# A graph layer with gathered rows: the first set's sorting spread over the table and the first fourteen parts

## The chip, the cores and the metric

The kernel runs on one core of one Trainium2 chip. The metric is device time in microseconds (us), the median of several runs. The engines are named as in the profile: PE is TensorE, DVE is VectorE, ACT is ScalarE, POOL is GpSimd, and SP is the engine that here only issues DMAs. PEld is PE's weight load.

## What is computed

The graph has 12,500 nodes with 128 features and 412,500 directed edges, sorted by destination. Each edge gets a weight from the difference of its ends; each node sums its weighted differences, adds a term in its in-degree, and the result is normalized.

```python
theta = x[dst] - x[src]
w = sigmoid(relu(theta @ W1 + b1) @ W2 + b2)
agg = segment_sum(w * theta, dst)
indeg = segment_sum(ones, dst)
out = layernorm(x + agg + indeg * (x @ W4 + b4))
```

## The kernel before

**Two stages.** The table stage computes `x @ W1` once for every node and writes rows of `x @ W1` and `x` side by side to DRAM (`z`). It walks over 14 chunks: twelve of 1,024 nodes, one of 128 and one of 84 (`table_chunk`, L598). For a chunk PE transposes eight tiles (L607), ACT copies them from PSUM (L610), PE multiplies (L612), DVE copies the product (L615), ACT copies `x` (L616), and SP writes the chunk to `z` (L617). The edge stage then walks over 372 parts of up to 1,024 edges, two parts to a block, so that a block shares a window of 96 destination nodes. I number parts and chunks from 0.

**A part.** POOL gathers the rows of the part's sources with eight indirect DMAs of 128 rows each (`gather`, L324 to L341; I call all eight "gather s"). Parts 0 to 7 (`NH` = 8) gather only `x`, so that they need not wait for `z`, and PE works out `x @ W1` for them in place (`both`, L728: transposes L735, ACT copies L737, products L740 and L742). Later parts gather from `z`. DVE forms one-hot matrices (L699 or L705 for the spreading of the window's values, L724 for the adding up), rectifies and reduces (L753 or L757 and L758, then L761), ACT forms the sigmoid and scales the rows (L762, L764), and PE adds them up by destination (L827). Per block, `window` (L651) and `part_y` (L664) compute the window's values: L655, L659, L660 and L672 on PE, copies L657, L662, L675 and L678 on ACT, L670, L676 and L680 on DVE.

**Gathers' pace.** There are nine row buffers (`zbuf`); two `x` parts share one. POOL takes the gathers strictly in order. Gathers 0 to 7 are held to the pace of the table. Gather 8 and later need all of `z`. Gathers 8 to 12 go into free buffers, gather 13 into the buffer of parts 0 and 1. From gather 14 on, each waits for a named PE instruction of the part six before it (`LAG` = 6): gather 14 for the last spreading matmul that part 8's turn issues (L714), and so on.

**Sorting.** Parts 0 to 17 (`PLAIN`) use the edges as they stand. The other parts are sorted in sets of 128 parts by the generator `place` (L425), which puts its work out in small steps; a `next(steps, None)` runs one. For one set there are 79 calls, in this order:

| calls | what they do | where |
|---|---|---|
| 1 | column constants | L434-449 |
| 2 to 4 | key, by thirds; each third holds the PSUM buffer `pw` | L453-464 |
| 5 to 7 | key, end | L467-479 |
| 8 to 23 | eight times the eight largest (L483), then their replacement (L485) | L481-485 |
| 24 | the list of frequent sources, its DMA on SP (L500), a matmul (L506) | L489-509 |
| 25 to 30 | counting, in sixths; each holds `pw` | L512-530 |
| 31 to 72 | shifting, 7 rounds of 6 strips; three DVE instructions a strip (L543, L545, L547) | L535-549 |
| 73, 74 | results out: DMA `off_d` (L557) on SP, three ACT copies | L551-565 |
| 75 to 79 | PE transposes (L571) and ACT copies (L573) into `src_i` and `rel` | L567-575 |

Set 0 holds parts 18 to 145. So gather 18 reads `src_i`, and part 18's one-hot reads `off_d` back from DRAM (`to_all`, L639).

**What sets the order.** All loops are unrolled. SP keeps the written order. For PE, DVE, ACT and POOL a scheduler fixes the order when the program is built, by its own estimate of when each instruction can run; on the chip every engine runs its list strictly in order. Buffers decide too: `pw` and `pd` are single PSUM buffers (2 KB a partition each), handed on in written order, and `pw` is used by the table's first four transposes, by `place`, by `window`, by `part_y` and by `both`. The strips' scratch `bits` (L205) lies in one PSUM tile, `fix`, with the row of numbers that L724 compares with and with `own` (written by ACT at L843, read by DVE at L848).

**Around the change.** Chunks 0 and 1 are emitted ahead of the loop at L914, so that loop runs for chunks 2 to 13. The loop over parts begins at L934; its line L944 decides how many steps of sorting each part carries.

Of the kernel before, what the change touches and what calls it, by code (L numbers as in the profile page):

```python
# [33 lines left out]
NH = 8  # L34
FIRST = P // K
MORE = 2
PLAIN = FIRST + MORE
# [11 lines left out]
def gnn_resnorm(  # L49
# [48 lines left out]
    chunks = [(n0, P, TC) for n0 in range(0, N - P * TC + 1, P * TC)]  # L98
# [34 lines left out]
    def load(i):  # L133

        s0, n, full = sets[i]
        es = ep.tile([P, CE], I32, name="es")
        ed = ep.tile([P, CE + 1], I32, name="ed")
        e0 = E1 + (s0 - PLAIN) * CE
        if full < n:
            nc.vector.memset(es[:n, :], 0)  # L140
            nc.vector.memset(ed[:n, :], N)
        for t, edges, m in ((es, src, CE), (ed, dst, CE + 1)):
            nc.sync.dma_start(t[:full, :m], bass.AP(
                tensor=edges.tensor, offset=edges.offset + e0, ap=[[CE, full], [1, m]]))
            if full < n:
                nc.sync.dma_start(
                    t[full:n, :TAIL], edges[E - TAIL:E].rearrange("(s e) -> s e", s=1))
        bb = ep.tile([P, 1], I32, name="bb")
        with nc.allow_non_contiguous_dma(reason="each block's first dst"):
            nc.sync.dma_start(bb[:n], bass.AP(  # L150
                tensor=dst.tensor, offset=dst.offset + e0, ap=[[SUB * CE, n // SUB], [0, SUB], [1, 1]]))
        return es, ed, bb
# [153 lines left out]
    def tiles(s):  # L306
        return K if s < NF else KT
# [16 lines left out]
    def gather(s):  # L324

        (src_i, _, _), i = set_of(s)
        for k in range(tiles(s)):
            ins = nc.gpsimd.indirect_dma_start(  # L328
                out=rows_of(s)[:, k, :], out_offset=None, in_=z if s >= NH else x,
                in_offset=IndirectOffsetOnAxis(ap=src_i[:, k, i:i + 1], axis=0))  # L330
            waits = [(gathers[-1], mybir.DependencyClass.NoSync)] if gathers else []
            at = (s * K + k) * 4 * len(chunks) // (NH * K) - 6
            if s < NH and 0 <= at < len(table_steps):
                waits.append((table_steps[at], mybir.DependencyClass.Sync))
            if s - LAG >= NH and (s - LAG, k) in steps_of:
                waits.append((steps_of[s - LAG, k], mybir.DependencyClass.Sync))
            for other, kind in waits:
                tc.add_manual_dep(
                    ins.ins, other.ins.name,
                    mybir.DependencyInfo(kind, mybir.DependencyReason.DATA), reason="gathers' pace")  # L340
            gathers.append(ins)  # L341
# [235 lines left out]
    with tc.manual_schedule(engines={SP}), tc.tile_pool(name="work", bufs=2) as wp, tc.tile_pool(  # L577
# [43 lines left out]
        @contextmanager  # L621
        def after(instructions):

            with ExitStack() as stack:
                for i in instructions:
                    stack.enter_context(tc.issue_after(i.ins))
                yield
# [23 lines left out]
        def window(b):  # L651

            d = blocks[b]
            pw = ps_l.tile([P, G, P], F32, name="pw")[:, 0, :]
            step(b * SUB - 4, 5, nc.tensor.transpose(pw[:, :WB], d["xw"][:WB], ident[:WB, :WB]))  # L655
            xwT = wp.tile([P, P], F32, name="xwT")
            nc.scalar.activation(xwT[:, :WB], pw[:, :WB], AF.Copy)  # L657
            pw = ps_l.tile([P, G, P], F32, name="pw")[:, :2, :]
            nc.tensor.matmul(pw[:WB], xwT[:, :WB], wts, start=True, stop=False)  # L659
            step(b * SUB - 4, 7, nc.tensor.matmul(pw[:WB, 1, :], ones_b[:, :WB], b4_3, start=False, stop=True))  # L660
            yu = yu_buf[b % len(yu_buf)]
            nc.scalar.activation(yu[:WB], pw[:WB], AF.Copy)  # L662
            d.update(u=yu[:, 1, :], yb=yu[:, 0, :])
            d["y3"] = part_y(b * SUB, SUB, d["yb"])  # L664
# [19 lines left out]
        def one_hot(s, half):  # L684


            n0, n1 = half * G, min(half * G + G, tiles(s))
            if half == 0:
                parts[s] = {"oh": oh_buf[s % 2]}
            oh = parts[s]["oh"]  # L690
            if s < PLAIN:
                (_, _, off), i = set_of(s)
                pd = ps_l.tile([P, G, P], F32, name="pd")
                pd = pd.rearrange("p k e -> p (k e)").bitcast(BF16)
                pd = pd.rearrange("p (k e) -> p k e", e=P)[:, :G, :]
                for k in range(n0, n1):
                    nc.tensor.transpose(pd[:, k - n0, :], off[:, k, i:i + 1].to_broadcast([P, P]),
                                        ident_b)
                nc.vector.tensor_scalar(oh[:3 * SW, n0:n1, :], pd[:3 * SW, :n1 - n0, :],  # L699
                                        place_c[:3 * SW], None, op0=OP.is_equal)  # L700
            elif half == 0:
                n = tiles(s)
                b, h = divmod(s, SUB)
                at = blocks[b]["to_all"].rearrange("p h (k e) -> p h k e", e=P)
                nc.vector.tensor_scalar(oh[:3 * SW, :n, :], at[:3 * SW, h, :n, :],  # L705
                                        place_c[:3 * SW], None, op0=OP.is_equal)
# [170 lines left out]
        def fetch(b):  # L877
            if b < NK:
                load_block(b)

        hot_blocks = range(PLAIN // SUB, NK)
        xts, done = [], []

        def chunk():
            c = len(done)
            xts.extend(table_load(i) for i in range(len(xts), min(c + 3, len(chunks))))
            done.append(table_chunk(c, xts[c]))
# [4 lines left out]
        def gather_first():  # L892

            while gathered[0] < AHEAD and (gathered[0] + 1) * len(chunks) <= (len(done) + 1) * NH:
                gather(gathered[0])
                gathered[0] += 1
# [17 lines left out]
        while len(done) < len(chunks):  # L914
            chunk()
            gather_first()
            with after(done[-1]):
                for _ in range(6):
                    next(steps, None)
        with after(done[7]):  # L920
            bases(FIRST, NS, ps_l)
# [12 lines left out]
        for s in range(NS + 2):  # L934
            if s in turns:
                edges[s + 3] = turns[s], load(turns[s])
            if s in edges:
                i, loaded = edges.pop(s)
                steps = place(i, ps_l, *loaded)
            if s == NH:  # L940
                nc.sync.dma_start(
                    hot_t, z[:HOT, :].rearrange("(p t) d -> p t d", t=HT))
                nc.scalar.activation(hot_t[:, :, :D], hot_t[:, :, :D], AF.Copy, scale=-1.0)
            if s % 2 == 0 or s < PLAIN - 3:  # L944
                for _ in range(3 if s < NH else 1):
                    next(steps, None)
            b = s // SUB
            if s % SUB == 0:
                fetch(b + 2)
                if b + 1 < NK:  # L950
                    window(b + 1)
            if s + AHEAD < NS:
                gather(s + AHEAD)
            if s >= NH and s + 2 < NS:
                one_hot(s + 2, 0)
            if s + 1 < NS:
                spread_y(s + 1)
            if s < NS - 1:
                one_hot_w(s)
            if s == NS - 2:  # L960
                one_hot_w(s + 1)
            if s < NS:
                weighted = weights(s)
            if s % SUB == 0 and b > 1:
                with after(weighted if s == NS else []):
                    normalize(b - 2)
            if s % SUB and b + 1 in hot_blocks:
                hot_weights(b + 1)
            if s < NH:
                one_hot(s + 2, 0)  # L970
            if s + 2 < NS and tiles(s + 2) > G:
                one_hot(s + 2, 1)
            if s % SUB == 0 and b + 1 in hot_blocks:
                hot_one_hot(b + 1)
            if s > 1:
                with after(weighted if s >= NS else []):
                    add_up(s - 2)
            if s % SUB == 0 and b + 1 in hot_blocks:
                hot_rows(b + 1)
            if s % 2 and s > PLAIN - 3:  # L980
                next(steps, None)
# [202 lines left out]
```

## Time and profile before

Three runs took 3914.03, 3919.13 and 3920.94 us. The profiled execution took 3919.01 us; its span, from the first instruction to the last, is 3917.2 us, so that 1.8 us lie outside.

| engine | busy us | share of the span | instructions |
|---|---|---|---|
| PE | 2667.6 | 68% | 15349 |
| PEld | 2252.2 | 57% | 15349 |
| DVE | 2829.5 | 72% | 5501 |
| ACT | 1594.4 | 41% | 5226 |
| POOL | 2866.5 | 73% | 2978 |

The mean granted PE clock is 0.81 of full speed. Some marks in the span, from the timelines of the engines:

| us from the span's start | what |
|---|---|
| 33.2 | DVE copies chunk 2 (L615) |
| 125.8 | DVE copies the last chunk (L615) |
| 136.3 | POOL issues the first DMA of gather 8 |
| 170.4 | ACT begins to read the sorted words (L565) |
| 179.9 | PE begins part 0 (L735) |
| 259.6 | POOL issues the first DMA of gather 14 |
| 301.6 | POOL issues the first DMA of gather 18 |
| 3889.4 | POOL issues the last DMA |

In the views, a line of a timeline gives start, duration, engine, line, operation, tiles and shapes, and in brackets the idle time before it with what ended it. A line of the waits gives the total, the number of times and the longest.

### The profile page before, as it was taken

To read this page: it belongs to the slowest core of one execution; us is meant where nothing else is said; L and a number is where in the kernel's file an instruction comes from. 1 tells how busy PE (TensorE), PEld (TensorE's weight loads), DVE (VectorE), ACT (ScalarE), POOL (GpSimd) and SP (SyncE) were. 2 spreads that over 40 slices of the span, in tenths; PEclk is the share of its full clock that TensorE was granted. 3 is DMA by queue.
4 is the path that set the end of the run, shared out by engine and by line. 5 is a ranking of instruction groups with operands and counts; after the bars stand their busy time and mean duration, and the time that the engine had idled before them with its cause. 6 is when DMAs were issued, how large, how long until landed. Compare 5 with 4: busy or idle time off the path is not lost.

```text
span 3917.2 us, 52459 instructions
## 1 busy us (share of the span) xinstructions
PE 2667.6 (68%) x15349; PEld 2252.2 (57%) x15349; DVE 2829.5 (72%) x5501; ACT 1594.4 (41%) x5226; POOL 2866.5 (73%) x2978
## 2 busy tenths in 40 slices
PE   3487776776667766667766776676766766767665
PEld 2366555555556655556555655566655656656554
DVE  6778787777767666669887777666666666666665
ACT  2254443434444343334444434444343443344443
POOL 3637777777777777777777777777777777777775
PEclk7698787877778888878887777878888888888887
DMA  5425444444444444445444444444445444444443
GB/s 179 138 66 163 138 138 142 142 144 143 139 143 143 142 143 142 133 143 150 143 140 138 142 141 146 142 139 139 141 142 144 142 141 138 142 143 144 141 136 98
DMA packets 242089, 547.83 MB, mean 140 GB/s; under 512 B 60819, under 2 KB 120893, under 8 KB 240129
## 3 DMA queue, kind: packets, MB, share of 16 engines
q0 software_dynamic: 141488, 385.15, 33.8%
q1 hardware_dynamic: 98335, 152.85, 12.9%
q10 hardware_dynamic: 1970, 6.40, 0.4%
q8 instruction: 123, 2.02, 0.2%
q14 instruction: 173, 1.42, 0.1%
HBM read 521.31 MB, written 22.85 MB: 139 GB/s over the span
## 4 chain that ended last, share of the span: by engine, by line
DVE 34%; DMA 22%; PE 19%; ACT 16%; issue 6%; POOL 2%; DVEq 0%; SPq 0%; ACTq 0%; POOLq 0%
DMA zbuf<-z,src_i 22%; PE pd L792 11%; ACT wx L764 10%; DVE ph L757 8%; DVE ph L758 8%; DVE lg L761 7%; PE pa L827 3%; ACT wx L762 2%; DVE of L779 2%; POOL zbuf L328 2%; DVE pw L676 1%; DVE ow L724 1%; PE pw L659 1%; ACT a L838 1%; DVE fix L848 1%
## 5 line engine op out<-in xcount | busy, mean ns | idle before, releaser
L328 POOL DMA_INDIRECT zbuf<-z,src_i x2825 | 2728.2, 966 | 860.9 <-issue 416.0
L792 PE MATMUL pd<-hot_t,of 128*128 128x256 f32 x3186 | 995.1, 482 | 187.5 <-DVE of L779 156.9
L757 DVE TENSOR_TENSOR ph<-ph,zbuf 128x1024 f32<-128x1024 f32 x364 | 446.7, 1227 | 846.3 <-DMA zbuf<-z,src_i 846.0
L792 PEld LDWEIGHTS pd<-hot_t,of 128*128 128x128 f32 x3186 | 777.8, 250 | 367.4 <-ACT wx L764 116.1
L827 PE MATMUL pa<-wx,ow 128*96 128x130 f32 x5938 | 905.6, 312 | 117.5 <-ACT a L838 109.3
L764 ACT ACTIVATE wx<-zbuf,wx 128x128 f32<-128x128 f32 x2969 | 910.8, 388 | 7.0
L827 PEld LDWEIGHTS pa<-wx,ow 128*96 128x96 f32 x5938 | 823.4, 192 | 153.6 <-ACT a L838 140.8
L714 PE MATMUL ph<-y,oh 128*128 128x128 bf16 x2905 | 292.5, 247 | 435.2 <-DVE y L680 287.6
L714 PEld LDWEIGHTS <-oh 128*128 128x128 bf16 x2905 | 236.4, 111 | 474.1 <-issue 342.1
L761 DVE TENSOR_REDUCE lg<-ph 128x8 f32<-128x1024 f32 x372 | 450.4, 1211 | 0.1
L758 DVE SCALAR_TENSOR_TENSOR ph<-ph,w_r 128x1024 f32<-128x1024 f32 x364 | 445.3, 1223 | 0.0
L838 ACT ACTIVATE a<-pa 96x130 f32<-96x130 f32 x186 | 50.4, 271 | 870.1 <-PE pa L827 870.0
L724 DVE TENSOR_TENSOR ow<-fix,rel 128x768 f32<-128x768 f32 x372 | 350.2, 942 | 12.0 <-ACT fix L843 5.9
L762 ACT ACTIVATE wx<-lg,b_c 128x8 f32<-128x8 f32 x372 | 112.2, 302 | 363.9 <-DVE lg L761 363.7
L779 DVE TENSOR_TENSOR of<-hot_all,fix 128x1152 f32<-128x1152 f32 x177 | 236.5, 1336 | 0.0
L678 ACT ACTIVATE ym<-pw 128x256 bf16<-128x256 f32 x186 | 70.6, 380 | 401.2 <-DVE pw L676 401.0
L827 PE MATMUL pa<-a,sh 96*96 96x130 f32 x370 | 87.5, 321 | 162.5 <-DVE sh L823 162.5
L705 DVE TENSOR_SCALAR oh<-to_all,place_c 123x1024 bf16<-123x1024 bf16 x354 | 169.9, 480 | 0.0
L672 PE MATMUL pw<-yu,pick 99*128 99x128 f32 x744 | 158.0, 335 | 13.1 <-ACT yu L662 5.8
L655 PE MATMUL pw<-ident,xw 96*128 96x96 f32 x186 | 54.8, 294 | 163.5 <-issue 120.5
L659 PE MATMUL pw<-wts,xwT 128*96 128x256 f32 x372 | 139.9, 462 | 37.6 <-ACT xwT L657 37.6
L827 PEld LDWEIGHTS pa<-a,sh 96*96 96x96 f32 x370 | 50.9, 174 | 191.6 <-DVE sh L823 189.4
(215 smaller groups left out, 2602.9 us busy)
## 6 DMA issues: line engine op xcount, KB each, us to landing
to_all<-off_d SPq DMA_DIRECT2D x177, 512.0 KB
zbuf<-z,src_i POOLq DMA_INDIRECT x2825
hot_all<-hot_d SPq DMA_DIRECT2D x177, 128.0 KB
z<-zbuf SPq DMA_DIRECT2D x12, 1024.0 KB
xw<-in_x_dram SPq DMA_DIRECT2D x186, 48.0 KB
out_dram<-o SPq DMA_DIRECT2D x186, 48.0 KB
zbuf<-in_x_dram ACTq DMA_DIRECT2D x12, 512.0 KB
zbuf<-z,src POOLq DMA_INDIRECT x80
```

Of the source, the lines that this page charges most:

```text
L328: ins = nc.gpsimd.indirect_dma_start(out=rows_of(s)[:, k, :], out_offset=None, in_=z if s >= NH else x, in_offset=IndirectOffsetOnAxis(ap= ...
L659: nc.tensor.matmul(pw[:WB], xwT[:, :WB], wts, start=True, stop=False)
L714: got = nc.tensor.matmul(d["ph"][:, k, :], d["oh"][:, k, :], blocks[b]["y3"][h], start=True, stop=True)
L724: nc.vector.tensor_tensor(ow, iota_f.to_broadcast([P, n, WB]), rel[:, :n, i:i + 1].to_broadcast([P, n, WB]), op=OP.is_equal)
L757: nc.vector.tensor_sub(ph, ph, zs[:, :n, :D])
L758: nc.vector.scalar_tensor_tensor(h[:, :n, :], ph, 0.0, w2_f.to_broadcast([P, n, D]), op0=OP.max, op1=OP.mult)
L761: summed = nc.vector.tensor_reduce(lg[:, :n], h[:, :n, :], AX.X, OP.add)
L762: nc.scalar.activation(wx[:, :n, D], lg[:, :n], AF.Sigmoid, bias=b2_c)
L764: scaled = nc.scalar.activation(wx[:, k, :D], xs[:, k, :], AF.Copy, scale=wx[:, k, D:D + 1])
L779: nc.vector.tensor_tensor(d["of"].rearrange("p t (h e) -> p t h e", e=HS), at[:, :, 0, :, :].to_broadcast([P, HT, SUB, HS]), nid.rearrange ...
L792: nc.tensor.matmul(d["px"], d["of"][:, t, :], hot_t[:, t, :], start=t == 0, stop=False)
L827: summed = nc.tensor.matmul(pa, one, w, start=h == 0 and i == 0, stop=h == 1 and i == len(terms) - 1)
```

## The change

Two numbers and two conditions change: how many steps of set 0's sorting are written behind each chunk of the table, and how many with each part.

```diff
@@ L914 @@
         while len(done) < len(chunks):
             chunk()
             gather_first()
             with after(done[-1]):
-                for _ in range(6):
+                for _ in range(2 if len(done) < len(chunks) else 4):
                     next(steps, None)
@@ L944 @@
             if s % 2 == 0 or s < PLAIN - 3:
-                for _ in range(3 if s < NH else 1):
+                for _ in range(4 if s < PLAIN - 4 else 1):
                     next(steps, None)
```

Before, twelve chunks carried 72 steps, through the last shifted strip, and parts 0 to 2 the remaining 7. Now eleven chunks carry 2 each and the last 4, in all 26: through the list of frequent sources and two sixths of the counting. Parts 0 to 13 then carry 4 each: the last four sixths with part 0, the strips with parts 1 to 11, and the end of the sorting with parts 11 to 13. Later sets carry one step a part as before.

## The prediction

> **What bounds the kernel now.** I read the page first, then POOL's timeline, then short windows and waits around POOL's longest stop.
>
> ```profile
> span 3917.2 us, 52459 instructions
> ...
> POOL 3637777777777777777777777777777777777775
> ...
> L328 POOL DMA_INDIRECT zbuf<-z,src_i x2825 | 2728.2, 966 | 860.9 <-issue 416.0
> ```
>
> POOL shows 73% busy, but 860.9 us idle over 2825 gather DMAs is 0.30 us each: its ordinary gap between two issues. From the fourth of the 40 slices on it issues without a real stop. POOL's timeline has the exceptions:
>
> ```profile
> 207.77 0.95 POOL L328 DMA_INDIRECT zbuf<-z,src  x1 [0.30 <-ACT txT L737]
> 259.56 0.95 POOL L328 DMA_INDIRECT zbuf<-z,src  x1 [50.84 <-ACT wx L764]
> 301.59 0.95 POOL L328 DMA_INDIRECT zbuf<-z,src_i  x1 [0.30 <-ACT wx L764]
> 3889.42 0.95 POOL L328 DMA_INDIRECT zbuf<-z,src_i  x1 [0.30 <-issue]
> ```
>
> Gather 14 begins at 259.56 after 50.84 us of waiting for part 8's turn. From there POOL needs 3889.42 - 259.56 = 3629.9 us for the remaining 2857 issues (371 parts of 8 and one of 1, less 14 x 8), 1.27 us each, 10.2 us a part, and 27.8 us of span follow. So the time is fixed by when POOL reaches its unbroken run. Line 301.59 is gather 18, the first to read `src_i`.
>
> Why does part 8 come so late? Windows of 25 us (PE, PEld, DVE, ACT, POOL busy; then PE clock, DMA share, GB/s):
>
> ```profile
> 150.00:175.00 25.00, 1.73 (x6) 1.10 (x7) 22.43 (x56) 3.87 (x5) 19.12 (x20) 0.50 0.39 110
> 200.00:225.00 25.00, 20.28 (x155) 16.23 (x154) 14.90 (x27) 15.54 (x47) 3.79 (x4) 1.00 0.21 72
> 225.00:250.00 25.00, 20.44 (x172) 17.40 (x172) 16.22 (x29) 11.86 (x33) 0.00 (x0) 1.00 0.02 5
> 275.00:300.00 25.00, 18.75 (x141) 15.06 (x139) 24.02 (x42) 13.29 (x46) 19.01 (x20) 0.80 0.47 134
> ```
>
> From 150 to 175 only DVE works, on sorting. From 200 to 250, in parts 0 to 7, DVE has 9 or 10 us free in 25. From 275, in parts 8 to 13, DVE is full already. The waits from 139 to 200 name the stop (total, times, longest):
>
> ```profile
> ACT es L565 <- DVE et L547: 33.7, 1, 33.7
> PE pw L571 <- ACT es L565: 31.5, 1, 31.5
> ```
>
> PE's list has the sort's transposes (L571) ahead of part 0, so PE stands for 31.5 us. The table is late for the same reason:
>
> ```profile
> 80.85 0.94 POOL L328 DMA_INDIRECT zbuf<-in_x_dram,src  x1 [16.21 <-PE pw L607]
> 103.54 0.94 POOL L328 DMA_INDIRECT zbuf<-in_x_dram,src  x1 [16.43 <-PE pw L607]
> ```
>
> POOL, paced by the table, stands still while DVE runs the maxima and the counting.
>
> **Prices.** A strip is three DVE instructions, 0.42 us apart (141.79, 142.21, 142.63, 143.06 in DVE's timeline), so 1.26 us, a round's last strip 0.8; the rounds of 6 take 6.9 to 7.7 us, so 42 strips cost 50 us. A sixth of the counting takes 2.68 (88.91 to 91.59). A maximum with its replacement takes 2.77 (61.01 to 63.78 in the same timeline). The change removes nothing: it takes 4 x 2.68 + 50 = 61 us of DVE work, 3 us of ACT and four groups of transposes out of the way of table and part 0, and sets them beside parts 0 to 13. I follow DVE's list of the changed program, with these durations.
>
> **Table.** Copy 2 stands at 33.2 as before. From it to the last copy the list holds 38.1 us of work (11 copies, the key, five maxima, five replacements). To this come waits. Chunks 3 and 4 each queue for `pw` behind a third of the key, and DVE's list has their copies ahead of the next third: each stalls DVE for transposes, copy and matmuls at the low clock, 44.51 to 50.13, some 5.8 us. Smaller ones: 0.7 for the edges' landing, about 4 until PE's pace catches up (3.5 us a chunk at 107 to 123). 33.2 + 38.1 + 16.5 = 88, against 125.8.
>
> **Table to part 0.** DVE's list then has three pairs (8.3), compares and the hot list (3.1), two sixths (5.3), the bases and checks (5.4 with PE's answer): 110. The first window and its values take 4 more. Then come four sixths with a first strip, 11.6: 125.5. They hold `pw`, which the second window needs; that takes 5.9, as at 174.04 to 179.91. Part 0 begins at 131.4, against 179.9, 48.5 earlier.
>
> **Parts 0 to 7.** From part 0 to gather 14 it took 79.65 us. PE's transposes of the sort at 187.3 to 191.3 leave this stretch: -4. Each block of 17.8 us gets some seven strips, 6.7 us of start-to-start DVE time onto 10.1. That is 16.8 of 17.8, so DVE isn't full, but it works in order. It used to wait in a block 1.72 (before L699), 2.34 (L753), 1.44 (L680) and 0.68 (L724), and the new list sets strips at about these points: five between the two L699, one behind L753, three before the next, four singles, five after L680. Overhang is about 2 us. Bounds: 0 a block if all of it fits, 6.7 if none does, and not below 0, since nothing is taken out of the blocks. I take 1.5, near the lower end, as the waits are rows of this stretch itself. Gather 14: 131.4 + 79.65 - 4 + 6 = 213, 46 earlier.
>
> **Parts 8 to 13, the new wait.** POOL's own pace would bring it to gather 18 at 213 + 32 x 1.27 = 254. But `src_i` isn't ready. From part 7's reduction to the last strip, DVE's list holds 50.3 us (18 of them strips) where DVE was full already; with 4 for waits the sort ends at 267.5. Then ACT reads the words (1.06 + 1.04 + 1.04), transposes and a copy follow: 271.5, against 301.6. Behind POOL's waiting gather 18 queue all later gathers, so this is where the path goes: 17 of the 46 us are given back. Gather 19 waits for part 14's spreading, whose y3 (L680) is 9.3 us of DVE list behind the sort, with perhaps 5 more of waiting; POOL gets there 11.4 after gather 18 begins, about when it is ready. Later parts take 6.6 us of DVE, under POOL's 10.2.
>
> **Queues passed.** SP: the list's DMA (L500) moves behind all writes of `z`, harmless; `off_d` (L557) now stands ahead of the windows of blocks 8 and 9 and of the first `to_all`, needed two parts later, 13 us at 6.6 us a part. The largest of these loads has 512 KB, at the windows' 142 GB/s 3.6 us, so I take nothing; without this cover it would be those 3.6 us once. POOL's list is unchanged. ACT's three copies stand among part 13's scalings: 3 us, no one waits but gather 18.
>
> **A rule against it.** The Trainium skill, SBUF — State Buffer, section "SBUF: two separate sides", says that a DMA issued by POOL cannot get its descriptors written while DVE runs an instruction in a two-port mode, and "Who interferes with whom" counts copies and tensor_scalar among those that can. The change puts strips beside 48 gathers of parts 8 to 13; one strip instruction of 0.42 us for each would be 20 us. The trace: from 139.5 to 170.1 DVE runs 76 instructions, nearly all strips, and POOL issues 25 DMAs in 30.6 us, 1.22 each, the pace it has everywhere. By the rule the time would be 3909, by the row 3889. I take the row, which is this very pair of instructions.
>
> **Sum.** 301.6 - 271.5 = 30 us; 3919.0 - 30 = 3889. The profiled run lies 0.1 from the median, so this serves for both.
>
> **Rivals.**
> All strips fit: blocks stay at 17.8, and DVE is full from 131.4 on. 112.8 us of list from the second block's y3 to the sort's end, 8 of waits, 4 to `src_i`: gather 18 at 256, time 3874. For: 16.8 of 17.8 fits on paper, and the scheduler placed the strips in gaps. [...]
> Nothing fits: 6.7 more a block, and the rest as above with 3 more waits: 213 + 21 + 61 = 295, time 3912. For: DVE stands on PE's path at L699 and L680.
> Slower: the strips' scratch shares the PSUM tile `fix` with `own`, so a strip can wait for ACT's L843, itself behind PE's adding up (L827), and everything on DVE stands behind that strip. Place: once a block, blocks 0 to 6. For: in the changed list the first strip after L724 waits for ACT. Against: L724 already waited for the same write, 0.68. It decides from 30 / 6.5 = 4.6 us a block beyond my sum; at 7 us, 45 us later, the time is 3934.
> No use: the time won is lost again past gather 18 (a late y3 or `to_all` stalls gathers 19 to 21 by 30 us), 3919. Against: POOL's slack there is about zero at gather 19, then grows 3 us a part.
>
> **Chances.** My sum 0.50 (3878 to 3902 on its own), all fits 0.20, nothing fits 0.14, no use 0.06, slower 0.10. A measurement of this kernel can tell about 0.2%, 8 us, from no change. "Nothing fits" at -7 lies on that line, so half of it counts as the same: faster 0.77, same 0.13, slower 0.10. The range 3870 to 3914 takes in all but the last two cases.
>
> **What would show it.** Last table copy near 88; part 0 near 131; gather 14 near 213; gather 18 waiting some 17 us for ACT's L573 and starting near 271; no other POOL stop after it; blocks of 17.8 + 1.5. I am wrong if blocks exceed 22 us, if the table is still paced by DVE waits past 100, or if POOL stops again after gather 18.

## The result, and the profile after

The changed kernel takes 3895.53 us, median of four runs (3893.75 to 3899.37), against 3920.03 for the kernel before in the same rounds (3914.03 to 3921.80): 24.5 us less, a ratio of 0.9942, 95% interval 0.9924 to 0.9959. The forecast was 3889, from 3870 to 3914. Between the profiled executions, span against span, it is 3917.2 - 3892.0 = 25.2 us. Most of the experiments below ran on other chips than this, on which every kernel, the one before too, takes 4840 to 4870 us; their totals are compared only with the kernel before on the same chip, and otherwise their traces are read, mostly up to gather 18.

The page after, in the same lines as before:

```profile
span 3892.0 us, 52446 instructions
...
POOL 6547777777777777777777777777777777777775
...
L328 POOL DMA_INDIRECT zbuf<-z,src_i x2825 | 2726.5, 965 | 860.5 <-issue 421.6
```

The first slice shows POOL at 6 tenths where it had 3: the table isn't paced by DVE's maxima any more. The gather DMAs cost what they did (965 ns and 0.30 us of gap). So the gain lies ahead of the unbroken run. POOL's timeline:

```profile
210.67 0.94 POOL L328 DMA_INDIRECT zbuf<-z,src  x1 [48.87 <-ACT wx L764]
265.01 0.94 POOL L328 DMA_INDIRECT zbuf<-z,src  x1 [26.56 <-PE pw L655]
278.83 0.95 POOL L328 DMA_INDIRECT zbuf<-z,src_i  x1 [0.30 <-DMA zbuf<-z,src]
3864.59 0.95 POOL L328 DMA_INDIRECT zbuf<-z,src_i  x1 [0.30 <-issue]
```

Gather 14 (210.67) comes 48.9 us earlier. But there is a second stop, which the kernel before doesn't have: 26.56 us, up to 265.01. Counting DMAs from 210.67, eight to a gather, that is the sixth DMA of gather 16. Gather 18 (278.83) doesn't wait at all, and is 22.8 us earlier than before; the last DMA is 24.8 us earlier. 26 of the 49 us were given back between gathers 14 and 18. The 2.1 us between 22.8 and 24.8 are the gather DMAs themselves, whose busy and idle times in the two pages differ by 1.7 and 0.4 us.

What was waited for is seen in PE's timeline:

```profile
256.67 1.11 PE L571 MATMUL pw<-ident,es 128*128 128x128 f32 x4 [1.34 <-ACT es L565]
...
260.37 0.60 PE L571 MATMUL pw<-ident,es 128*128 128x128 f32 x4
...
261.65 0.66 PE L571 MATMUL pw<-ident,ew 128*128 128x128 f32 x4 [0.46 <-ACT src_i L573]
263.01 0.66 PE L571 MATMUL pw<-ident,ew 128*128 128x128 f32 x4 [0.70 <-ACT rel L573]
...
264.50 0.25 PE L655 MATMUL pw<-ident,xw 96*128 96x96 f32 x1
```

These are the sort's four groups of transposes, and right behind them the transpose of window 7 (block 7, parts 14 and 15). Line 655 registers it as step 5 of part 10, and `gather` ties the sixth DMA of gather 16 to that step, six parts behind. The window has nothing to do with the sort; but both use the single `pw`, in written order, and all four groups (calls 75 to 78) are written in part 12 ahead of window 7. The 25 us windows (PE, PEld, DVE, ACT, POOL; PE clock, DMA share, GB/s) show what the sort's end itself waited for:

```profile
150.00:175.00 25.00, 20.39 (x162) 16.88 (x161) 20.43 (x50) 15.34 (x45) 9.06 (x10) 1.00 0.33 108
200.00:225.00 25.00, 18.81 (x130) 15.65 (x131) 21.38 (x44) 13.87 (x47) 9.45 (x10) 0.81 0.18 50
225.00:250.00 25.00, 12.81 (x76) 10.71 (x74) 25.00 (x51) 8.99 (x30) 10.39 (x11) 0.57 0.22 64
250.00:275.00 25.00, 18.45 (x124) 15.63 (x124) 17.35 (x43) 13.71 (x33) 7.63 (x8) 0.81 0.32 88
```

From 150 to 175, where PE worked for 1.73 us before, it now works for 20.39, at the full clock, beside the strips. From 225 to 250, in the parts behind part 7, DVE is full to the last hundredth. PE and ACT wait for it: in this window ACT 7.7 us for DVE's L761 and PE 7.0 for its L699.

### The profile page after: what moved, and what is told of

It reads as the page before. It is cut to its first block, busy times and chain, and to the rows that moved or that the text cites. A ratio compares the mean times of both kernels' runs of the same rounds, so it can differ in the third digit from the quotient of the medians.

```text
span 3892.0 us, 52446 instructions
## 1 busy us (share of the span) xinstructions
PE 2679.7 (69%) x15349; PEld 2257.9 (58%) x15349; DVE 2821.8 (73%) x5501; ACT 1593.6 (41%) x5226; POOL 2865.2 (74%) x2978
## 4 chain that ended last, share of the span: by engine, by line
DVE 33%; DMA 23%; PE 21%; ACT 15%; issue 6%; POOL 2%; SPq 0%; DVEq 0%; ACTq 0%; POOLq 0%
DMA zbuf<-z,src_i 21%; PE pd L792 13%; ACT wx L764 10%; DVE ph L757 8%; DVE ph L758 7%; DVE lg L761 6%; PE pa L827 3%; DVE of L779 2%; POOL zbuf L328 2%; ACT wx L762 2%; DVE ow L724 1%; DVE pw L676 1%; PE pw L659 1%; ACT a L838 1%; DVE fix L848 1%
## 5 line engine op out<-in xcount | busy, mean ns | idle before, releaser
L792 PE MATMUL pd<-hot_t,of 128*128 128x256 f32 x3186 | 1014.8, 490 | 183.8 <-DVE of L779 154.6
L792 PEld LDWEIGHTS pd<-hot_t,of 128*128 128x128 f32 x3186 | 792.1, 255 | 369.2 <-ACT wx L764 113.0
L827 PE MATMUL pa<-wx,ow 128*96 128x130 f32 x5938 | 895.1, 310 | 117.9 <-ACT a L838 105.7
L827 PEld LDWEIGHTS pa<-wx,ow 128*96 128x96 f32 x5938 | 813.5, 190 | 152.7 <-ACT a L838 136.1
L714 PE MATMUL ph<-y,oh 128*128 128x128 bf16 x2905 | 291.8, 246 | 442.5 <-DVE y L680 286.5
L714 PEld LDWEIGHTS <-oh 128*128 128x128 bf16 x2905 | 235.6, 111 | 481.0 <-issue 349.7
L761 DVE TENSOR_REDUCE lg<-ph 128x8 f32<-128x1024 f32 x372 | 450.4, 1211 | 0.0
L838 ACT ACTIVATE a<-pa 96x130 f32<-96x130 f32 x186 | 50.3, 270 | 877.0 <-PE pa L827 877.0
L724 DVE TENSOR_TENSOR ow<-fix,rel 128x768 f32<-128x768 f32 x372 | 350.3, 942 | 8.2 <-ACT fix L843 7.6
L827 PE MATMUL pa<-a,sh 96*96 96x130 f32 x370 | 87.9, 322 | 151.8 <-DVE sh L823 151.6
L655 PE MATMUL pw<-ident,xw 96*128 96x96 f32 x186 | 54.9, 295 | 177.7 <-issue 127.0
L672 PE MATMUL pw<-yu,pick 99*128 99x128 f32 x744 | 156.3, 331 | 11.5 <-ACT yu L662 5.4
L827 PEld LDWEIGHTS pa<-a,sh 96*96 96x96 f32 x370 | 51.7, 177 | 180.5 <-DVE sh L823 177.8
```

The costliest lines, as they stand in the source:

```text
L714: got = nc.tensor.matmul(d["ph"][:, k, :], d["oh"][:, k, :], blocks[b]["y3"][h], start=True, stop=True)
L724: nc.vector.tensor_tensor(ow, iota_f.to_broadcast([P, n, WB]), rel[:, :n, i:i + 1].to_broadcast([P, n, WB]), op=OP.is_equal)
L761: summed = nc.vector.tensor_reduce(lg[:, :n], h[:, :n, :], AX.X, OP.add)
L792: nc.tensor.matmul(d["px"], d["of"][:, t, :], hot_t[:, t, :], start=t == 0, stop=False)
L827: summed = nc.tensor.matmul(pa, one, w, start=h == 0 and i == 0, stop=h == 1 and i == len(terms) - 1)
```

## The experiments

The theory after the result: the time follows the start of POOL's run, and what sets it now is the pace entry of window 7, standing behind the sort's end through `pw`, with DVE full ahead of that. The rivals: strips are dear in the blocks of parts 0 to 7; or the stop is only the first of several that are equally late.

On the slower chips part 0 begins anywhere from 177 to 192 us for reasons that no edit explains, so the table counts from there. The ratio is that of the medians of all runs; the times are those of one profiled execution, in us, and the last three columns are measured from the start of part 0 (PE's L735) to the start of the gather, or of the last strip's last instruction.

| kernel | ratio to the kernel before, interval | part 0 | gather 14 | last strip | gather 18 |
|---|---|---|---|---|---|
| changed kernel | 0.9974 (0.9957 to 0.9990) | 183.70 | 82.8 | 138.8 | 163.6 |
| window first | 0.9955 (0.9938 to 0.9972) | 177.28 | 84.2 | 151.4 | 154.4 |
| window first, again | 0.9966 (0.9949 to 0.9983) | 180.47 | 86.5 | 154.4 | 157.4 |
| window first, third | 0.9959 (0.9942 to 0.9976) | 178.23 | 84.4 | 152.4 | 155.5 |
| no pace entry | 0.9935 (0.9910 to 0.9959) | 186.95 | 83.9 | 140.4 | 145.0 |
| seven a part | 0.9986 (0.9971 to 1.0001) | 191.89 | 119.3 | 88.9 | 169.9 |
| seven a part, again | 1.0001 (0.9988 to 1.0013) | 182.25 | 120.4 | 89.9 | 171.1 |
| two, then seven | 0.9974 (0.9954 to 0.9993) | 186.93 | 82.0 | 153.4 | 173.3 |
| seven a part, pace from 24 | 0.9987 (0.9974 to 1.0000) | 184.60 | 37.1 | 92.6 | 143.2 |
| pace from 24 alone | 0.9999 (0.9983 to 1.0016) | 192.49 | 37.5 | 145.4 | 150.4 |

**The changed kernel as the anchor.** No edit.

> The changed kernel itself, unedited, as the anchor for the edits of it: the first two calls ran all kernels, the one before too, at some 4850 us instead of 3919, with PE's and DVE's rows full of idle time that ends in nothing the profile shows. If that holds here too, POOL is not what sets the pace of the later parts, an earlier start of POOL's run is still a shift of the whole, and the ratio should be that of the result, 0.994 (0.990 to 0.997), between the window-first edit (0.9955, 0.9966) and the front-loaded one (0.9986, 1.0001). If the run is at some 3895 again, ratio 0.992 to 0.996, POOL's long stop of some 27 us for L655 near 265. Rival for the slow runs (the gain depends on POOL's issues being the bound): ratio 1.000.

4853.51 us against 4866.20, ratio 0.9974: 12.7 us less, half the gain of the first chip. 1.000, the rival, is excluded, but the ratio also lies just outside the expected 0.990 to 0.997, and the interval meets the first chip's only at its end. The stop is the same one, and longer:

```profile
333.44 0.95 POOL L328 DMA_INDIRECT zbuf<-z,src  x1 [35.28 <-PE pw L655]
```

**Taking the entry away.** Window 7's two pace entries aren't made; every other order stays.

```diff
-            step(b * SUB - 4, 5, nc.tensor.transpose(pw[:, :WB], d["xw"][:WB], ident[:WB, :WB]))
+            moved = nc.tensor.transpose(pw[:, :WB], d["xw"][:WB], ident[:WB, :WB])
+            if b != 7:
+                step(b * SUB - 4, 5, moved)
```

and the same for L660.

> The changed kernel without the two pace entries of window 7 (L655 and L660 for block 7), so that gathers 16's last three DMAs no longer wait for them; the computation and the order of all other engines stay. Theory: POOL goes straight on to gather 18, which now waits for `src_i` (261.6) and, with its third DMA, for the values of window 7 (L672, 266.6): POOL's run starts some 15 us earlier, span 3877 (3872 to 3882), and a stop '<- ACT' at L573 or '<- PE' at L672 takes the place of '<- PE pw L655'. Rival, the stop at L655 is only the first of several equal ones: gather 18 starts at 275 or later, span 3888 or more.

POOL runs on from gather 16 to gather 18, and stops there (lines behind L660 stand four lower in this kernel, so its L676 is L672):

```profile
317.72 0.95 POOL L328 DMA_INDIRECT zbuf<-z,src  x1 [0.30 <-ACT wx L768]
331.93 0.94 POOL L328 DMA_INDIRECT zbuf<-z,src_i  x1 [13.27 <-ACT src_i L573]
...
338.92 0.95 POOL L328 DMA_INDIRECT zbuf<-z,src_i  x1 [4.80 <-PE pw L676]
```

The stop for L655 is gone, and the two that were named in advance took its place, 13.27 for `src_i` and 4.80 for the window's values. From the start of part 0 gather 18 comes 18.6 us earlier than in the anchor. Gather 19, behind the second stop, is still 16.0 us earlier, near the 15 expected. This shows the cause of the stop: nothing but the two entries differs, and the traces have every engine's instructions in the same order as in the changed kernel. The total, 4843.33, is the best ratio of these chips, 0.9935; its interval just meets the anchor's. This edit has no run on a chip like the first, so the total that it would bring there is not shown.

**Window first.** A part's calls of the sort behind the next block's window.

```diff
-            if s % 2 == 0 or s < PLAIN - 3:
-                for _ in range(4 if s < PLAIN - 4 else 1):
-                    next(steps, None)
             b = s // SUB
             if s % SUB == 0:
                 fetch(b + 2)
                 if b + 1 < NK:
                     window(b + 1)
+            if s % 2 == 0 or s < PLAIN - 3:
+                for _ in range(4 if s < PLAIN - 4 else 1):
+                    next(steps, None)
```

> The changed kernel with the sort's calls of a part put behind the next block's window instead of ahead of it; nothing else differs. Theory: after the change POOL's long stop (26.56 us, up to 265.01) is the pace set on window 7's transposes (L655), which stand on PE behind the sort's last transposes only because both use the one `pw` in written order. With the window first, that stop goes from gather 16; DVE's work of one window moves ahead of the last strips, so the sort ends some 3 us later, `src_i` comes near 265, gather 18 waits for it and starts there instead of at 278.83: span 3892 - 14 = 3878 (3870 to 3885). Rival, DVE full in parts 8 to 13 is what holds every key there: gather 18 starts near 279 as before, span 3892 within 4.

> The kernel of the first experiment (a part's calls of the sort behind the next block's window) once more, because the chip of the first call ran every kernel, the one before too, at some 4870 us. Theory, where POOL's issues set the pace again: no stop at gather 16 for L655, a stop of about 10 us at gather 18 for `src_i` (L573), gather 18 at about 265 instead of 278.83, span 3878 (3870 to 3885), ratio to the kernel before about 0.990. Rival (DVE full in parts 8 to 13 holds every key there): gather 18 near 279, span 3892, ratio 0.994.

> The window-first edit a third time, since the call before ran again at some 3917 us for the kernel before. There the late-moves kernel started gather 18 at 278.95, as the changed kernel does (278.83), with its stop at gather 14 instead of gather 16: a stop that is moved is worth nothing if another key of the pace takes its place. Theory: with window 7 ahead of the sort's transposes and the strips where they were, the stop at gather 16 goes, the keys of part 8 and 9 aren't late, and gather 18 waits for `src_i` alone: it starts at 260 to 267, span 3874 to 3882, ratio 0.990. Rival (some other key of the pace is late by about as much, as in the late-moves kernel): gather 18 at 275 or later, ratio 0.994 or 0.995.

These are three chips, and none on which POOL sets the pace of the later parts, so the span that was expected was never put to the test. The order of the waits was: in all three the stop for L655 is gone from gather 16 and one for `src_i` stands at gather 18, as here in the third:

```profile
333.68 0.95 POOL L328 DMA_INDIRECT zbuf<-z,src_i  x1 [16.07 <-ACT src_i L573]
```

But the sort ends 13 to 16 us later than in the anchor, not 3: the edit changes what the scheduler puts on DVE's list, by more than one window's work. So gather 18 gains only 6 to 9 us, where 14 were expected. Medians are 4841.02, 4841.65 and 4839.54.

**The strips elsewhere.** Seven calls a part in the first eight parts, or two there and seven in parts 8 to 13.

```diff
-                for _ in range(4 if s < PLAIN - 4 else 1):
+                for _ in range(7 if s < NH else 1):
```

```diff
-                for _ in range(4 if s < PLAIN - 4 else 1):
+                for _ in range(2 if s < NH else 7 if s < PLAIN - 4 else 1):
```

> The changed kernel with the same calls of the sort ending by part 7: seven a part in the first eight parts, none in parts 8 to 13. Theory: DVE had about 4.3 of 25 us free beside the strips in parts 0 to 7; 21 more calls (some 23 us of DVE) fill that and lengthen these four blocks by 10 to 16 us in all, so gather 14 starts at 221 to 227; but then nothing holds POOL any more up to gather 18, which starts 42 us later at 263 to 269: span 3876 to 3883. Rival, strips among the blocks of parts 0 to 7 are the dear ones (they stand ahead of what PE waits for): blocks lengthen by 10 us each, gather 14 at 250, gather 18 at 292, span 3905.

> Seven calls a part in the first eight parts, none after, once more on a chip where POOL's issues set the pace. Theory: gather 14 at 221 to 227 (210.67 in the changed kernel), no stop of POOL after it, gather 18 at 263 to 269: span 3876 to 3883. Rival, strips in the blocks of parts 0 to 7 are the dear ones: gather 14 at 250, gather 18 at 292, span 3905. The first call's look speaks for the rival: gather 14 stood at 311 there, after 95 us of waiting, against 261 to 271 in the other three kernels.

> The changed kernel with the sort's calls moved the other way: two a part in the first eight parts, seven in parts 8 to 13, ending in part 13 as before. Theory: gather 14 comes some 4 us earlier (206), which is worth nothing, as the end of the sort decides: 16 more calls, some 19 us of DVE, now lie where DVE is full, so the sort ends 15 to 19 us later, window 7 behind it, and POOL's long stop ends near 282: span 3907 to 3911. Rival, what the strips add to the blocks of parts 0 to 7 decides: span 3888 or less.

Seven a part: 4868.05 and 4856.47 us. The theory expected a gain of 12 us or so and is wrong here: gather 14 comes 37 us later. But the rival's mechanism, strips that cost 10 us in each block, isn't what the trace shows. The first four blocks begin 22.3, 22.6 and 53.6 us apart in the second run; the changed kernel has 21.3, 24.3 and 18.9 on these chips. The loss lies in one block, the third. PE's timeline there:

```profile
255.84 3.75 PE L827 MATMUL pa<-wx,ow 128*96 128x130 f32 x16 [7.13 <-DVE ow L724]
266.30 3.78 PE L827 MATMUL pa<-wx,ow 128*96 128x130 f32 x16 [6.70 <-DVE ow L724]
...
272.26 1.11 PE L571 MATMUL pw<-ident,es 128*128 128x128 f32 x4 [1.75 <-ACT es L565]
274.82 0.42 PE L655 MATMUL pw<-ident,xw 96*128 96x96 f32 x1 [1.45 <-ACT src_i L573]
...
280.70 0.66 PE L735 MATMUL pw<-ident,zbuf 128*128 128x128 f32 x2 [1.99 <-issue]
```

The sort's first group of transposes stands on PE ahead of window 4 and of part 6's L735, all in `pw`, and DVE has to finish the strips first. Seven calls a part are not seven strips in each part: 24.7 of the 42 strips lie in this block of DVE's list, against 7.3 in the changed kernel, and DVE is busy for 43.3 of the 53.6 us. It is the wait that took 31.5 us in the kernel before, now ahead of part 6 instead of part 0.

Two, then seven: 4856.08 us. Gather 14 gains 0.8 us (4 expected), the last strip comes 14.6 us later (15 to 19 expected), POOL's stop is 45.76 us long and gather 18 starts 9.7 us later. So in the trace the sort's end decides, as the theory has it. The total doesn't decide between theory and rival: its ratio, 0.9974, is the anchor's, and 10 us is hardly more than the half widths of the two intervals, 8 and 9.5 us.

**Strips early, transposes late.** The strips with parts 0 to 7, but the sort's calls behind the last strip (73 on) held until part 9's weights are issued, and written behind window 6. And the same with the pace of gathers begun with gather 24.

```diff
-            if s % 2 == 0 or s < PLAIN - 3:
-                for _ in range(4 if s < PLAIN - 4 else 1):
+            if s < NH:
+                for _ in range(6 if s < NH - 1 else 4):
                     next(steps, None)
...
+            if s == NH + 2:
+                with after(weighted):
+                    for _ in range(8):
+                        next(steps, None)
+            elif s >= PLAIN - 4 and (s % 2 == 0 or s < PLAIN - 3):
+                next(steps, None)
```

```diff
-            if s - LAG >= NH and (s - LAG, k) in steps_of:
+            if s >= 24 and (s - LAG, k) in steps_of:
```

> The changed kernel with six calls a part in parts 0 to 6 and four in part 7, so that all strips are written by part 7, and with the sort's last calls (reading of the words, PE's transposes L571) held until part 9's weights are issued and behind window 6. It tells two readings of the front-loaded kernel apart, whose first three blocks took 21 to 23 us like those of the changed kernel, while the fourth took 53. Theory: what cost there was not seven strips a part, but PE standing at the sort's transposes ahead of part 6; with these later, no block is longer than in the changed kernel of the slow chips (21, 24, 19 us), gather 14 starts near 266 to 272 (266.47 there), the sort ends 10 to 15 us earlier, the stop for L655 shrinks from 35 us to 20 or less, and gather 18 starts at 325 to 335 (347.3 there): ratio to the kernel before 0.993 to 0.996 (0.9974 there). Rival, the strips themselves lengthen the blocks: gather 14 at 285 or later, gather 18 at 345 or later, ratio 0.998 or more.

> The same kernel, and the pace of gathers begun with gather 24 instead of 14. Theory: with neither window 7's transposes nor part 8's weights to wait for, gathers 14 and 15 go out early, gather 16 waits for the buffer that parts 6 and 7 give back (near 265 to 275), and gather 18 waits for `src_i` only: 310 to 320 (347.3 in the changed kernel on the slow chips), and unless later parts lose it again, a ratio of 0.989 to 0.993. Rival: the front-loaded kernel with this pace started gather 18 some 30 us before the same kernel with the old pace, and had lost most of that by gather 32; if the parts behind can't keep up, the ratio is that of the late-moves kernel, within 0.001.

These two ran on a chip like the first one: 3917.17 us for the kernel before. The first of the two takes 3899.35 us, ratio 0.9950 (0.9933 to 0.9966), the second 3870.31, ratio 0.9877 (0.9860 to 0.9893). The figures expected were those of the slower chips; here the changed kernel's first profile is the yardstick. With six calls a part and PE free of the transposes, the blocks begin 22.2, 18.5 and 24.3 us apart (21.5, 17.9, 18.9 there): the first two are 0.6 to 0.7 longer and the third, with 8.7 strips, 5.4, against 35 with the transposes and 24.7 strips in it. Gather 14 starts 5.4 us later. The first kernel still gains nothing by it:

```profile
240.29 0.94 POOL L328 DMA_INDIRECT zbuf<-z,src  x1 [18.90 <-ACT yu L662]
...
278.95 0.94 POOL L328 DMA_INDIRECT zbuf<-z,src_i  x1 [0.30 <-issue]
```

The stop has moved from gather 16 to the fourth DMA of gather 14, and gather 18 starts within 0.2 us of where it did. DVE is as full as before, 23.54 us of the 25 from 225 on, and ACT stood 16.3 us there for PE's L827, which waited for DVE's L724 among the strips. By the code (`add_up`), the fourth DMA of gather 14 is tied to the adding up of part 6, which is this L827; it ends at 239.54:

```profile
235.76 3.78 PE L827 MATMUL pa<-wx,ow 128*96 128x130 f32 x16 [2.04 <-DVE ow L724]
239.58 0.31 ACT L762 ACTIVATE wx<-lg,b_c 128x8 f32<-128x8 f32 x1 [16.33 <-PE pa L827]
```

So another pace entry had taken the place of window 7's. The expectation, a shorter stop and an earlier gather 18, failed: the last strip came 5.6 us earlier, not 10 to 15, and a stop that is moved was worth nothing. In the second kernel the pace is gone up to gather 23. Gathers 15 and 16 wait 10.62 and 11.06 us, while the parts whose buffers they take are still at work, and then only `src_i` is left:

```profile
247.41 0.94 POOL L328 DMA_INDIRECT zbuf<-z,src_i  x1 [17.99 <-ACT src_i L573]
```

Gather 18 starts 31.5 us earlier than in its twin, and the kernel takes 29.0 us less: on such a chip the time does follow the start of POOL's run. It beats the kernel before by 46.9 us on the chip where it was measured, and the changed kernel, which has no run on that chip, by its ratio (0.9877 against 0.9942).

**The pace alone.** Two kernels have the later pace without the late transposes.

> Seven calls a part in the first eight parts, and the pace set on gathers (no nearer than six parts behind the work) begun with gather 24 instead of 14, so that gathers 14 to 23 wait only for a free buffer and for `src_i`. Theory (the start of POOL's unbroken run is all that counts): gathers 14 to 17 go out beside parts 3 to 8, gather 18 as soon as part 9 has given its buffer back and `src_i` is there, 232 to 250: span 3845 to 3863. Rival: the pace was no limit of its own, as parts 8 to 14 are no faster than one per 10.2 us beside the gathers, and POOL stops again behind them: gather 18 early but stops of 15 us or more later, span 3876 or above.

> The changed kernel with only the pace of gathers begun with gather 24 instead of 14; its sort and the order of PE, DVE and ACT stay. It divides the gain of the kernel with both edits (ratio 0.9877, gather 18 at 247.41) between them. Theory: `src_i` is then the only thing gather 18 waits for, and it comes as in the changed kernel, 259 to 262: gather 18 there, 17 to 20 us earlier than 278.83, span 3872 to 3876, ratio 0.989 to 0.990. Rival: the earlier gathers take something from parts 0 to 8 (a port, the memory, the order of waits), blocks lengthen, `src_i` comes at 270 or later, ratio 0.992 or more.

Both ran on the slower chips, and the totals, 4847.61 and 4862.10 us, show no gain over the anchor. With seven a part, gather 18 starts 20.4 us earlier than in the anchor, short of the 29 or more expected, and POOL stops again behind it, 15.14 us at gather 24, as the rival has it; gather 32 is back behind the anchor's (341.9 against 338.7 us from the start of part 0). With the changed kernel's sort gather 18 starts 13.2 us earlier, and the third block takes 29.6 us instead of 18.9, though the traces have every engine's instructions in the same order:

```profile
342.90 0.95 POOL L328 DMA_INDIRECT zbuf<-z,src_i  x1 [33.66 <-ACT src_i L573]
```

So `src_i` is what it waits for, as the theory has it, but the parts come later, as the rival has it. In the late-moves pair, on a chip like the first, the same edit of the pace lengthened no block (third block 23.7 us, 24.3 in the twin), so the rival may hold for the slower chips only. How much the pace alone would bring on a chip like the first is open.

## Why the prediction was right, and where it was off

The time came out 6.5 us above the forecast, and its chain is the one that the traces show: an earlier table, an earlier part 0, an earlier start of POOL's run, and a part of the gain given back behind the sort's end. One step failed, and that the sum is still this near is in part luck.

*Table.* The last copy stands at 88.5; the forecast was 88. POOL's stops for L607 are down to 9.75 and 4.48 us.

*Table to part 0.* Part 0 begins at 133.75; the forecast was 131.4. The second window does stand behind the four sixths of the counting, in `pw`, as written:

```profile
127.21 0.39 PE L655 MATMUL pw<-ident,xw 96*128 96x96 f32 x1 [10.71 <-DVE bad L532]
```

*Parts 0 to 7.* The forecast was 19.3 us a block and gather 14 at 213. The first block took 21.5 (26.5 before), the next two 17.9 and 18.9, and gather 14 started 18.7 us into the fourth, at 210.67. The strips cost 2.2 us in the last three, not 4.5. Here "all strips fit" was nearer than my 1.5, and "nothing fits" and the slower rival, a strip standing for L843 in every block, didn't happen.

*Parts 8 to 13.* This is the step that failed. I wrote that gather 18 would be the one to wait, some 17 us for `src_i`, and that no other stop of POOL would follow. The sort ended earlier than I summed, and `src_i` was complete at 261.6, 17 us before gather 18:

```profile
254.76 0.17 DVE L547 COPY_PREDICATED et<-fix,ew 128x12 f32<-128x12 int32 x1
261.00 0.60 ACT L573 ACTIVATE src_i<-pw 128x512 int32<-128x512 f32 x1 [0.66 <-PE pw L571]
```

The last strip ends at 254.9, forecast 267.5. Part 7's reduction, from which I counted, ended at 208.6 instead of 213.2; DVE's list behind it took 45.7 us instead of 50.3, and its waits 0.6 instead of 4.

The stop was 26.56 us, at gather 16, for window 7's transpose. That a wait would give back part of the gain, and that the sort's end would set it, was right; 26 us were given back instead of 17, because the queue past which the sort's end was moved was not only gather 18's: I looked up which engines' lists the sort's transposes stood in, and passed over which buffer they hold. `pw` was in my reasons for the table and for part 0, and not for part 12. Nor did I go through all pace entries of parts 8 to 13, only that of L714. The experiment without the two entries shows it, on a slower chip. The place of the stop costs more than its lateness: it ends only 3.4 us after `src_i` is complete, but 11 DMAs of gathers 16 and 17, 13.8 us, still stood behind it, which in my sum were issued before the wait.

The two errors have opposite signs. With the sort as early as it came, gather 18 could have started near 261.6, 9.9 us before the forecast of 271.5; the stop at gather 16 put it 17.2 us later, at 278.8. What is left is 7.3 us, about what the time differs by, 3895.5 against 3889. That they nearly cancel is luck. Nor would 261.6 have been the whole of it: without the entries a second stop of 4.80 us followed at gather 18's third DMA, for the window's values. "No use" was the nearest rival in kind, a loss further down, but it was placed behind gather 18.

*The rule against the change* (the Trainium skill, SBUF — State Buffer, "SBUF: two separate sides") was rightly set aside for these strips: from 213.77 to 237.51 POOL issues 20 DMAs, 1.25 us each, while DVE is busy for 23.56 of 23.74 us, strips among its work. The row doesn't refute the rule: the page's "Who interferes with whom" counts a `tensor_scalar` only when its operands meet the conditions of the two-port mode, which the prediction left out, and the strips keep their scratch in PSUM.

## What to carry to other kernels

When the end of a piece of work is moved, list not only the engines' queues it now stands in, but every single buffer it holds on the way and everyone written behind it in that buffer; then look for pace entries and waits tied to those. Find what the fixed-rate engine waits for in each of the parts in between, not only at the first use of the result. And moving a stop to an earlier gather was worth nothing here, since the same full engine lay behind both: the late transposes alone started gather 18 at 278.95, as the changed kernel does, and with the pace gone as well at 247.41.

## What was not expected of the hardware

The same program ran some 25% longer on a slower chip, 4853.51 against 3895.53 us, and four chips in all ran the kernel before at 4857 us or more. It isn't the granted clock alone (0.733 against 0.801). PE's idle time ahead of L792, the changed kernel on the first chip and on a slower one:

```profile
L792 PE MATMUL pd<-hot_t,of 128*128 128x256 f32 x3186 | 1014.8, 490 | 183.8 <-DVE of L779 154.6 <-ACT wx L764 29.0
```

```profile
L792 PE MATMUL pd<-hot_t,of 128*128 128x256 f32 x3186 | 1125.4, 502 | 528.0 <-issue 426.3 <-ACT wx L764 50.9 <-DVE of L779 41.0
```

On the slower chip 426.3 us of idle time end in nothing the profile shows. From the start of one L792 to the next, with no other matmul between, more than 1 us passes 294 times, 543 us in all; on the first chip never. POOL then takes 12.6 us a part instead of 10.2, with waits, so it isn't what sets the pace there. Single instructions take what they take on the first chip: the median transpose L735 273 ns on both, the median last instruction of a strip into `et` 384 ns against 382.

One pair of runs gives a hint. In the anchor the third block takes 18.85 us, as on the first chip, with no gather beside it and the DMA engines at 0.01 of their time. With the pace begun at gather 24, on another of the slower chips and with the same order on every engine, 12 gather DMAs fall into this block, the DMA share is 0.20, and it takes 29.6 us. In the pair on the chip like the first, the block takes 24.3 us without gathers beside it and 23.7 with them, at a DMA share of 0.35. So the delay may come with the gathers' traffic. But in "two, then seven" the second block takes 18.4 us on a slower chip at a DMA share of 0.27, so traffic alone doesn't decide it, and the cause isn't settled. It means that a gain at POOL's start need not show in the total on such a chip.

On the chip of the late-moves pair a gather DMA took 969 ns in the fastest kernel against 965 in the changed kernel's first profile, with no gap over 0.5 us in either after gather 18: 10.4 us over 2825 DMAs. That is where its 31.4 us of lead over the changed kernel at gather 18 became 20.7 us of span. Its twin with the old pace, on the same chip, has 968, so the later pace isn't the cause; whether the chip or the moved sort is stays open.
